# A decoder layer on one core: outer sums by quarters, experts of two tiles side by side, output weights loaded from ScalarE's queue

## The chip, the cores and the metric

The kernel runs on one core of one Trainium2 chip. A core has TensorE (matmuls), VectorE and ScalarE (elementwise work, both read the matmul banks), GpSimd (elementwise work between on-chip buffers) and SyncE, which here only issues DMAs. Each engine works through its own list of instructions in order and waits on semaphores for the others. In the profile they are PE (with PEld for its weight loads), DVE, ACT, POOL and SP. The metric is the device time of one execution in microseconds, lower is better. Everything is float32.

## The reference

The input is 2048 tokens (32 sequences of 64) of 512 numbers. Three blocks follow each other, each on a normalised copy of its input, each added to its input:

```python
# 1: self-attention, 32 heads of 128
q = (hidden_states @ Wq + bq).reshape(b, n, H, HD)      # k, v alike
q = rmsnorm(q, gq); k = rmsnorm(k, gk)
scores = jnp.einsum('bnhd,bmhd->bhnm', q, k) * scale
attn = jax.nn.softmax(scores, axis=-1)
out = jnp.einsum('bhnm,bmhd->bnhd', attn, v).reshape(b, n, H * HD)
return out @ Wo + bo
...
# 2: cross-attention of channels (64 by 64 weights) to a context of 128
energy = jnp.einsum('bcn,bcm->bnm', q, k) / scale
x = jnp.einsum('bnm,bcm->bcn', jax.nn.softmax(energy, axis=-1), v)
return skip + x
...
# 3: 8 of 64 experts
scores = jax.nn.softmax(flat @ router_weight.T + router_bias)
topk_w, topk_idx = jax.lax.top_k(scores, 8)
out = flat * topk_w.sum(-1, keepdims=True) + w_dense @ expert_bias
```

`w_dense` holds the eight chosen weights of a token in a row of 64, zeros elsewhere.

## The kernel before

A tile is 128 tokens (two sequences); there are 16. The big matrix products are computed with Strassen's scheme (Winograd's form): a product of two 2x2 block matrices takes seven block products, numbered 1 to 7, instead of eight, at the price of sums of blocks before and after.

**First half: attention (0 to about 1380 us).** The heads go in 16 groups of two, the tiles in two halves of eight, and of each half two units of four tiles. Two of the group passes (the first group of each half) use one level of the scheme (`single`); the other 30 are *windows* (class `Window`), which use two levels. A window computes q and k of two heads for its two units by four *outer* steps n = 0 to 3, over the outer products (1, 5), (2, 6), (7, 3) and (4,); each outer step runs the seven inner products in up to four places m = 0 to 3 (`outer`, products at L655). VectorE or ScalarE empties a finished bank into the buffer `qk` (first contents L666, L669, L676; additions L679). `qk` of a unit has four places (h, ab) for the two heads and the two kinds of token tile, and in each place j = 0 is q and j = 1 is k. After outer step 2, two *outer sums* bring the places into their final form, `add` at L734: (1, 0) += (1, 1), then (1, 1) += (0, 1), over 128x512, for unit 0 on GpSimd and for unit 1 on VectorE. Outer step 3 then writes over (0, 1). The dictionary `behind` (L737) says after which (n, m) these sums and the squares for the q and k norms (ScalarE, L356) are issued. Between the places m, `plan` puts the value products (`v`, products at L387 into the banks va and vb, copies on ScalarE L403, sums on VectorE L407), the scaling of q and k of the window before (GpSimd L542, VectorE L544), the transposes of the probabilities, and at the end scores (L555), mix (L592) and store (L607) of units already scaled. The weights of the next window are loaded by SP (L107) and their sums made on GpSimd, `more_sums` being the last (L152 to L155), by calls of `make` placed in the dictionary `more`.

In this half the order on VectorE, ScalarE, GpSimd and TensorE is that of the program text. A small list, `waiting`, holds VectorE work (L544, parts of a softmax) that is issued at the next place.

**Passage (about 1380 to 1430).** The attention output of each tile (32 heads of 128) is multiplied by Wo. `load_wo` (L804) brings Wo in eight pieces of 1 MB: the four of its left column at the start of the last window, the four of the right column after it, each as soon as a buffer is free. `wo_sums` makes Wo's block sums in eight steps on VectorE (L860), one at a time, when the generator `making_wo` is advanced. `first_out` is the first pair of tiles: its token sums (L886) are in the dictionary `sums`, by step. `drain` runs the steps: one step is four of the 16 accumulating matmuls of a product, each two instructions (so four steps a product, 28 for the pair); after given numbers of steps it issues the last transposes, scalings and scores of the attention. The last attention units are finished between them.

**Second half: output pairs (about 1430 to 1923).** The other seven pairs run in `strassen_out` (products at L837), again 28 steps a pair; the last pair has its own branch. After each step `advance` moves the *tails* of the pair before on: each tile's cross-attention (`cross_attention`, L1041) and experts (`experts`, L1107) are a generator, and a `yield k` in it means "go on k + 1 steps later". A tail ends with the transpose of the expert weights (L1143), the product with the 64 expert rows (`pm`, L1148, which contracts over 128 rows of which 64 are zero in `eb_sb` and `wds`), an addition (L1149) and the store of the tile (L1150). The odd tile of a pair starts later than the even one. The residual tiles x live in four buffers from their load to their store, so a pair's load of x waits for a store of the pair two before. The matmul banks come from three pools: `ps_a` with three banks (output products, L1095/L1097 and `pm`), `ps_t` with two, `ps_s` with three. In this half only TensorE has the program's order; the others are ordered by the scheduler of the language.

## Time and profile before

| what | us |
|---|---|
| median of 3 runs (1923.52 to 1924.39) | 1923.66 |
| the profiled execution | 1925.16 |
| its span, first to last instruction | 1923.3 |
| TensorE busy | 1878.1 |
| VectorE busy | 1232.1 |
| GpSimd busy | 1042.6 |
| ScalarE busy | 647.7 |
| one window (start to start) | 42.3 |
| one middle output pair (start to start) | 62.26 |

Busy time of TensorE is modelled from the starts of pipelined matmuls, so short refills after a wait count as busy; the distance from start to start is the safer measure. A row of the order in time gives the start in us, the duration, engine, line, operation, result and sources, the shapes and how many instructions were merged; in brackets stand the idle time before it and what ended it. A row of the waits gives who waited for whom, the total, how many times and the longest. The granted TensorE clock is 1.00 of full speed in the windows and in the middle pairs, 0.94 from 1380 to 1430 and 0.93 from 1846 to 1923.

### The profile page before, as it was taken

The page shows a single profiled execution, that of the slowest core. Times are in us where ns is not written, and L with a number is a line of the kernel's source. Part 1 is how long each engine was busy: PE and PEld are TensorE (multiplying, and loading weights), DVE is VectorE, ACT ScalarE, POOL GpSimd, SP SyncE. Part 2 cuts the span into 40 slices and gives each one's busy share as a digit, 9 for nine tenths or more (in the row PEclk, how much of TensorE's full clock was granted, in tenths as well). Part 3 has the DMA queues.
Part 4 walks back from the last instruction along what each step waited for, and adds up shares of the span by engine and source line. Part 5 has one row for each costly group of instructions (what it writes and reads, how often), then busy time and mean ns, then how long its engine had stood idle before and what let it go on. Part 6 is the DMA issues. An engine that isn't in the chain of part 4 may idle for free.

```text
span 1923.3 us, 40481 instructions
## 1 busy us (share of the span) xinstructions
PE 1878.1 (98%) x16845; PEld 1615.8 (84%) x16845; DVE 1232.1 (64%) x2034; ACT 647.7 (34%) x1580; POOL 1042.6 (54%) x814
## 2 busy tenths in 40 slices
PE   9999999999999999999999999999989999999997
PEld 8888888888888888888888888888877888888875
DVE  6866777766666658766666676666663545554555
ACT  2344334344433343344433343443311212221122
POOL 5856666666567639766566766655234323331320
PEclk9999999999999999999999999999999999999998
DMA  4234434333343343333443333344925231223100
GB/s 138 67 125 140 131 113 133 122 105 112 126 130 109 111 143 101 111 100 106 128 132 111 111 109 102 100 127 134 301 74 182 91 111 68 69 91 113 44 25 22
DMA packets 164567, 214.90 MB, mean 112 GB/s; under 512 B 10144, under 2 KB 135136, under 8 KB 160288
## 3 DMA queue, kind: packets, MB, share of 16 engines
q1 hardware_dynamic: 163200, 211.24, 34.1%
q8 instruction: 132, 2.16, 0.5%
q10 hardware_dynamic: 1184, 1.08, 0.2%
q14 instruction: 51, 0.42, 0.1%
HBM read 171.92 MB, written 40.37 MB: 110 GB/s over the span
## 4 chain that ended last, share of the span: by engine, by line
PE 74%; DVE 12%; POOL 7%; issue 3%; DMA 2%; ACT 1%; SPq 0%; POOLq 0%; DVEq 0%; ACTq 0%
PE p_w L655 24%; PE py L837 17%; PE va L387 7%; PE vb L387 6%; POOL qk L734 5%; PE ms_w L779 3%; PE o L592 3%; PE s L555 3%; DVE qk L666 3%; DVE qk L679 3%; DVE qk L544 2%; PE pt_p L249 1%; DMA x<-in_x_dram 1%; PE pa L445 1%; DVE sums L262 1%
## 5 line engine op out<-in xcount | busy, mean ns | idle before, releaser
L655 PE MATMUL p_w<-x,w 128*128 128x256 f32 x2940 | 723.9, 383 | 8.9 <-DVE qk L666 8.4
L655 PEld LDWEIGHTS p_w<-x,w 128*128 128x128 f32 x2940 | 521.2, 190 | 71.0 <-DVE qk L666 13.0
L666 DVE TENSOR_TENSOR qk<-p_w,qk 128x512 f32<-128x512 f32 x360 | 212.7, 599 | 136.5 <-PE p_w L655 100.6
L356 ACT ACTIVATE sq<-qk 128x512 f32<-128x512 f32 x256 | 158.1, 628 | 399.2 <-POOL qk L734 225.1
L387 PEld LDWEIGHTS va<-w,x 128*128 128x128 f32 x2048 | 263.6, 191 | 30.5 <-ACT v L403 20.5
L387 PE MATMUL va<-w,x 128*128 128x128 f32 x2048 | 276.1, 278 | 2.1 <-ACT v L403 2.1
L679 DVE TENSOR_TENSOR qk<-p_w,qk 128x512 f32<-128x512 f32 x360 | 220.1, 620 | 58.4 <-PE p_w L655 54.9
L120 POOL TENSOR_TENSOR w<-w 128x768 f32<-128x768 f32 x126 | 245.3, 1958 | 2.4
L265 POOL TENSOR_TENSOR prob<-prob,inv 128x512 f32<-128x512 f32 x64 | 78.7, 1230 | 298.2 <-DVE inv L264 295.0
L542 POOL TENSOR_TENSOR qk<-qk,rs 128x512 f32<-128x512 f32 x128 | 174.6, 1364 | 101.7 <-DMA rs<-row_w 89.3
L837 PE MATMUL py<-wo,a 128*128 128x256 f32 x992 | 227.5, 381 | 0.4 <-DVE wo L860 0.4
L837 PEld LDWEIGHTS py<-wo,a 128*128 128x128 f32 x992 | 183.7, 190 | 32.3 <-issue 7.3
L387 PEld LDWEIGHTS vb<-w,x 128*128 128x128 f32 x1536 | 201.4, 192 | 9.7
L387 PE MATMUL vb<-w,x 128*128 128x128 f32 x1536 | 202.4, 275 | 0.0
L403 ACT COPY v<-va 128x256 f32<-128x256 f32 x256 | 95.0, 371 | 311.7 <-PE va L387 311.5
L544 DVE SCALAR_TENSOR_TENSOR qk<-qk,gqk,rs 128x512 f32<-128x512 f32 x128 | 171.7, 1342 | 3.9 <-DMA rs<-row_w 2.3
L837 PE MATMUL py<-wo_t,a 128*128 128x256 f32 x672 | 154.7, 381 | 0.0
L837 PEld LDWEIGHTS py<-wo_t,a 128*128 128x128 f32 x672 | 125.2, 190 | 17.3 <-issue 0.8
L734 POOL TENSOR_TENSOR qk<-qk 128x512 f32<-128x512 f32 x60 | 90.7, 1512 | 61.1 <-DVE qk L679 58.7
L407 DVE TENSOR_TENSOR v<-vb,v 128x256 f32<-128x256 f32 x192 | 80.7, 420 | 45.7 <-PE vb L387 27.2
L257 DVE TENSOR_REDUCE mx<-s 128x8 f32<-128x512 f32 x64 | 44.1, 689 | 96.4 <-PE s L555 96.4
L607 ACT ACTIVATE ot<-o,bvt 128x256 f32<-128x256 f32 x256 | 99.4, 470 | 2.2 <-PE o L592 2.2
(193 smaller groups left out, 2227.5 us busy)
## 6 DMA issues: line engine op xcount, KB each, us to landing
rs<-row_w SPq DMA_DIRECT2D x120, 512.0 KB
mixed<-ot SPq DMA_DIRECT2D x64, 512.0 KB
a<-mixed SPq DMA_DIRECT2D x32, 1024.0 KB
w<-in_wq_dram SPq DMA_DIRECT2D x64, 256.0 KB
w<-in_wk_dram SPq DMA_DIRECT2D x62, 256.0 KB
w<-in_wv_dram SPq DMA_DIRECT2D x62, 256.0 KB
wo<-in_wo_dram SPq DMA_DIRECT2D x8, 1024.0 KB
x<-in_x_dram SPq DMA_DIRECT2D x20, 256.0 KB
```

The costliest lines, as they stand in the source:

```text
L120: on.tensor_tensor(*(it.rearrange("p c j d -> p (c j) d") for it in (out, a, b)), ALU.subtract)
L356: nc.scalar.activation(sq, of, AF.Square)
L387: nc.tensor.matmul(to[:, j, :], left[i][:, c, j, :], right[i][:, c, 2, :], start=first and j == 0 and c == 0, stop=c == 1, skip_group_chec ...
L403: nc.scalar.copy(self.v[h, ab], what)
L542: nc.gpsimd.tensor_tensor(k, k, rk, ALU.mult)
L544: lambda: nc.vector.scalar_tensor_tensor(q, q, gqk, rq, ALU.mult, ALU.mult)
L607: nc.scalar.activation(ot[:, h, :, b * SEQ : (b + 1) * SEQ], o[b][:, h, :, :], AF.Identity, bias=bvt[:, hg * HG + h : hg * HG + h + 1],)
L655: nc.tensor.matmul(bank[:, s, :], self.w.inner[o][i], inner_x[self.half, o][i], start=first and s == 0, stop=True, skip_group_check=True,)
L666: nc.vector.tensor_tensor(to(t, j), bank, add(t, j), ALU.add)
L679: nc.vector.tensor_tensor(to(t, j), bank, to(t, j), ALU.add)
L734: on.tensor_tensor(qk[to], qk[to], qk[what], ALU.add)
L837: nc.tensor.matmul(py, a[:, g, :], b[g // KH][:, g % KH, :], start=n == 0 and g == 0, stop=n == last and g == NHG - 1,)
```

## The change

Outer sums: each sum is cut by j into two of 128x256, and each is issued at a place of its own. For unit 0 (GpSimd) the j = 0 pair comes after (2, 1) and the j = 1 pair after (2, 2); for unit 1 (VectorE) the four quarters are spread over (2, 2), (2, 3) and (3, 0). The squares of the second head move back by up to one place. In the windows, the last two calls of `make` move from (2, 3) to (3, 0), and in the windows of group 1 one call of `inner` from (2, 1) to (2, 2).

Passage: the eight loads of Wo are issued by ScalarE instead of SP. Wo's sums are formed in another order (t2 from the new b12, then t1 from t2) and issued after the steps 8, 10, 14, 15, 16, 18, 21 and 22 instead of 9 to 16. In the first pair, product 6 comes before product 5, the token sums are formed with other operands, the addition of product 1 to xa moves behind product 2, and the transposes and scalings are issued after other numbers of steps.

Output pairs: the pair sums on GpSimd (L1008, L1009, in the last pair L969) move to VectorE. Six of the small loads before the first pair (`xw` of v and skip, router weights and bias, and the expert rows, now loaded twice, into rows 0 to 63 and 64 to 127) are issued by ScalarE; the two memsets of GpSimd fall away. The tails have other yields. For the first seven pairs, the even tile stops after it has chosen its experts and the odd tile does the rest for both: one transpose of both tiles' weights side by side (128 x 128), two products over 64 rows each, two additions, two stores. The tiles of the last pair each do their own, over 64 rows.

```diff
@@ -216,6 +216,10 @@
         tc.keep_in_program_order(nc.sync.dma_start(out=to, in_=what))
+    def load_beside(to, what):
+        nc.scalar.dma_start(out=to, in_=what)
     def statistics(xs, name, on_gpsimd=False):
...
@@ -728,25 +732,34 @@
...
                 )
-            def add(t, to, what):
-                qk = units[t].qk
+            def add(t, j, to, what):
+                to, what = (units[t].qk[it][:, j, :] for it in (to, what))
                 on = nc.vector if t else nc.gpsimd
-                on.tensor_tensor(qk[to], qk[to], qk[what], ALU.add)
+                on.tensor_tensor(to, to, what, ALU.add)
             behind = {
                 (1, 3): lambda: [squares(0, 0, t) for t in range(2)],
+                (2, 1): lambda: (
+                    add(0, 0, (1, 0), (1, 1)),
+                    add(0, 0, (1, 1), (0, 1)),
+                ),
                 (2, 2): lambda: (
-                    add(0, (1, 0), (1, 1)),
-                    add(0, (1, 1), (0, 1)),
-                    squares(1, 0, 0),
+                    add(0, 1, (1, 0), (1, 1)),
+                    add(0, 1, (1, 1), (0, 1)),
+                    add(1, 1, (1, 0), (1, 1)),
                 ),
                 (2, 3): lambda: (
-                    add(1, (1, 0), (1, 1)),
+                    add(1, 1, (1, 1), (0, 1)),
+                    add(1, 0, (1, 0), (1, 1)),
+                    squares(1, 0, 0),
                     squares(1, 1, 0),
+                ),
+                (3, 0): lambda: (
+                    add(1, 0, (1, 1), (0, 1)),
                     squares(1, 0, 1),
                 ),
-                (3, 0): lambda: add(1, (1, 1), (0, 1)),
                 (3, 1): lambda: squares(1, 1, 1),
...
@@ -803,10 +816,11 @@
...
             it = it.rearrange("p (g f) -> p g f", f=DH)
-            nc.sync.dma_start(
+            nc.scalar.dma_start(
                 out=it,
...
@@ -861,12 +875,14 @@
...
             for half in range(2):
-                subtract(t1[half], b12[half], b11[half])
-                yield
                 subtract(b12[half], b22[half], b12[half])
...
             for half in range(2):
-                subtract(t2[half], b22[half], t1[half])
+                nc.vector.tensor_tensor(t2[half], b12[half], b11[half], ALU.add)
+                yield
+            for half in range(2):
+                subtract(t1[half], b22[half], t2[half])
                 yield
...
@@ -886,9 +902,9 @@
...
         sums[3] = combine(ALU.add, s1, a21, a22)
-        sums[4] = combine(ALU.subtract, a21, a11, a21)
-        sums[5] = combine(ALU.subtract, a11, s1, a11)
-        sums[6] = combine(ALU.subtract, s4, a12, a11)
+        sums[4] = combine(ALU.subtract, a11, s1, a11)
+        sums[5] = combine(ALU.subtract, s4, a12, a11)
+        sums[7] = combine(ALU.subtract, a21, a22, a11)
         def product(i, it):
...
@@ -900,26 +916,26 @@
...
         nc.scalar.copy(p1, py)
-        nc.gpsimd.tensor_tensor(la, la, p1, ALU.add)
         yield
...
         add(la, py)
+        nc.gpsimd.tensor_tensor(la, la, p1, ALU.add)
         yield
...
         add(lb, py)
-        add(rb_, py)
-        yield
-        py = yield from product(5, s1)
-        add(ra, py)
         add(rb_, py)
...
             nc.gpsimd.tensor_tensor(to, to, p1, ALU.add)
+        yield
+        py = yield from product(5, s1)
+        add(ra, py)
+        add(rb_, py)
         add_bias(xa)
...
@@ -966,7 +982,7 @@
...
             nc.vector.tensor_tensor(s2, s1, a11, ALU.subtract)
-            nc.gpsimd.tensor_tensor(a21, a11, a21, ALU.subtract)
+            nc.vector.tensor_tensor(a21, a11, a21, ALU.subtract)
             py = yield from product(2, a12)
...
@@ -1005,9 +1021,9 @@
...
         nc.vector.tensor_tensor(lb, lb, py, ALU.add)
-        nc.gpsimd.tensor_tensor(a22, a21, a22, ALU.add)
-        nc.gpsimd.tensor_tensor(a21, a11, a21, ALU.subtract)
-        yield
+        nc.vector.tensor_tensor(a22, a21, a22, ALU.add)
+        yield
+        nc.vector.tensor_tensor(a21, a11, a21, ALU.subtract)
         py = yield from product(1, a11)
...
@@ -1038,7 +1054,8 @@
...
         done(tb, xb)
-    def cross_attention(t, xt):
+    def cross_attention(t, xt, apart):
         name = f"x{t}"
@@ -1052,7 +1069,7 @@
...
         nc.scalar.copy(kvs, kv)
-        yield 1
+        yield apart
         halves = [slice(b * SEQ, (b + 1) * SEQ) for b in range(2)]
...
@@ -1104,10 +1121,12 @@
...
         nc.vector.tensor_tensor(xt, xt, py, ALU.add)
+    chosen_by = {}
     def experts(t, xt):
...
         xn = layernorm(xt, name)
-        yield 4
+        yield 3
         ft = work.tile([P, KC, P], F32, tag="ft", name=f"ft_{name}", bufs=1)
...
@@ -1132,27 +1151,44 @@
...
         nc.vector.tensor_tensor(chosen, lg, rest, ALU.not_equal)
-        wd = wds[:, t % 2, 0:NEXP]
+        alone = t >= NT - 2
+        side = 0 if alone else t % 2
+        if side:
+            wds, other = chosen_by.pop(t - 1)
+        else:
+            wds = work.tile([P, 2, NEXP], F32, tag="wds", name=f"wds_{name}")
+        wd = wds[:, side, :]
         nc.vector.scalar_tensor_tensor(wd, ex, inv, chosen, ALU.mult, ALU.mult)
...
         nc.vector.scalar_tensor_tensor(xt, xn, ws, xt, ALU.mult, ALU.add)
-        yield 4
+        if not alone and not side:
+            chosen_by[t] = wds, xt
+            return
+        yield 3
+        n = NEXP if alone else 2 * NEXP
         pw = ps_t.tile([P, P], F32, tag="pt", name=f"pw_{name}")
-        nc.tensor.transpose(pw, wds[:, t % 2, :], ident)
+        nc.tensor.transpose(pw[0:n, :], wds.rearrange("p a e -> p (a e)")[:, 0:n], ident)
         wt = work.tile([P, P], F32, tag="wt", name=f"wt_{name}")
-        nc.scalar.copy(wt, pw)
+        nc.scalar.copy(wt[0:n, :], pw[0:n, :])
         yield 1
-        pm = ps_a.tile([P, D], F32, tag="pa", name=f"pm_{name}")
-        nc.tensor.matmul(pm, wt, eb_sb, start=True, stop=True)
-        nc.vector.tensor_tensor(xt, xt, pm, ALU.add)
-        nc.sync.dma_start(out=out_flat[bass.ts(t, P), :], in_=xt)
+        both = [(t, xt)] if alone else [(t - 1, other), (t, xt)]
+        pms = [ps_a.tile([P, D], F32, tag="pa", name=f"pm{i}_{name}") for i in range(len(both))]
+        for i, pm in enumerate(pms):
+            rows = slice(i * NEXP, (i + 1) * NEXP)
+            nc.tensor.matmul(pm, wt[rows, :], eb_sb[rows, :], start=True, stop=True)
+        for (at, it), pm in zip(both, pms):
+            nc.vector.tensor_tensor(it, it, pm, ALU.add)
+            nc.sync.dma_start(out=out_flat[bass.ts(at, P), :], in_=it)
     def after_attention(t, xt):
-        if t % 2 and t < NT - 1:
-            yield 2
-        yield from cross_attention(t, xt)
+        second = t % 2 and t < NT - 1
+        if second:
+            yield 0
+        yield from cross_attention(t, xt, 3 if second else 1)
         yield from experts(t, xt)
@@ -1346,7 +1382,7 @@
...
                 (1, 3): [lambda: make(1)],
-                (2, 3): [lambda: make(2)],
+                (3, 0): [lambda: make(2)],
             }
...
@@ -1360,7 +1396,7 @@
...
                     ((1, 2), 4),
-                    ((2, 1), 4),
+                    ((2, 2), 4),
                 ):
...
@@ -1434,14 +1470,14 @@
...
                     sums[done]()
-                elif done >= 9:
-                    next(making_wo, None)
-
-        go(2)
+                elif done in (8, 10, 14, 15, 16, 18, 21, 22):
+                    next(making_wo)
+        go(3)
         line.turn()
...
         line.scale()
-        go(4)
+        go(3)
         line.scale()
...
@@ -1475,17 +1511,15 @@
...
             half = slice(b * SEQ, (b + 1) * SEQ)
-            load(xw[half, j, half], src)
+            (load if j < 2 else load_beside)(xw[half, j, half], src)
     rwt = work.tile([P, KC, NEXP], F32, tag="rwt", name="rwt", bufs=1)
-    load(rwt, rw_t.rearrange("(kc p) e -> p kc e", p=P))
+    load_beside(rwt, rw_t.rearrange("(kc p) e -> p kc e", p=P))
     rb_b = work.tile([P, NEXP], F32, tag="rb", name="rb_b", bufs=1)
-    load(rb_b, rb.partition_broadcast(P))
+    load_beside(rb_b, rb.partition_broadcast(P))
     eb_sb = work.tile([P, D], F32, tag="eb", name="eb_sb", bufs=1)
-    wds = work.tile([P, 2, P], F32, tag="wds", name="wds", bufs=1)
-    nc.gpsimd.memset(eb_sb[NEXP:P, :], 0.0)
-    nc.gpsimd.memset(wds, 0.0)
-    load(eb_sb[0:NEXP, :], eb)
+    for half in range(2):
+        load_beside(eb_sb[half * NEXP : (half + 1) * NEXP, :], eb)
     for n in range(6):
...
```

## The prediction

> **What bounds the kernel now.** I read the page first, then the waits, then the order in time of one late window, of the passage between the two halves of the kernel, and of the last pair.
>
> ```profile
> span 1923.3 us, 40481 instructions
> ...
> PE 1878.1 (98%) x16845; PEld 1615.8 (84%) x16845; DVE 1232.1 (64%) x2034; ACT 647.7 (34%) x1580; POOL 1042.6 (54%) x814
> ```
>
> TensorE is busy 98% of the span, so a faster VectorE, ScalarE or GpSimd is worth only the gaps it closes in TensorE's row. The busy sum leaves 45 us, and short refills after a wait hide a little more. The waits of the weight loads show the gap that repeats:
>
> ```profile
> PEld va L387 <- ACT v L403: 20.5, 60, 1.5
> PEld p_w L655 <- DVE qk L666: 13.0, 31, 1.0
> ```
>
> There are 30 windows, so 60 and 31 waits are two and one in each. TensorE's order of time in one window:
>
> ```profile
> 1285.37 1.03 PE L655 MATMUL p_w<-x,w 128*128 128x256 f32 x4
> 1286.36 1.16 PE L387 MATMUL va<-w,x 128*128 128x128 f32 x8
> 1287.74 1.13 PE L655 MATMUL p_w<-x,w 128*128 128x256 f32 x4 [0.22 <-DVE qk L666]
> 1288.72 1.16 PE L387 MATMUL va<-w,x 128*128 128x128 f32 x8
> 1289.72 1.03 PE L655 MATMUL p_w<-x,w 128*128 128x256 f32 x4
> 1290.58 1.05 PE L387 MATMUL vb<-w,x 128*128 128x128 f32 x8
> ```
>
> Read the starts. Undisturbed, four p_w take 0.87 from start to start and eight v products 0.89, so from 1285.37 to 1290.58 the rows need 4.39; they take 5.21. The loss is 0.82 us, 0.49 of it ahead of 1287.74. What stands there, on VectorE and on GpSimd:
>
> ```profile
> 1285.41 0.69 DVE L734 TENSOR_TENSOR qk<-qk 128x512 f32<-128x512 f32 x1
> 1287.26 0.42 DVE L666 TENSOR_TENSOR qk<-p_w,qk 128x256 f32<-128x256 f32 x1 [1.16 <-POOL qk L734]
> ```
>
> ```profile
> 1284.12 3.11 POOL L734 TENSOR_TENSOR qk<-qk 128x512 f32<-128x512 f32 x2 [2.16 <-DVE qk L679]
> 1287.19 1.00 POOL L152 TENSOR_TENSOR w<-w 128x384 f32<-128x384 f32 x1
> ```
>
> GpSimd's two outer sums end at 1287.23; only then may L666 overwrite what they read, and TensorE needs the bank that L666 empties.
>
> **A. Outer sums by quarters (30 windows).** Each 128x512 sum becomes two of 128x256. GpSimd pays a little more (rows of 128x256 on it follow each other every 0.70: L960, three in 2.09), so 2.8 for 3.1 with less waiting. Its first two quarters move in front of the last products of the window's third group, into its idle 2.16. The later two start at 1284.1 as now, behind one VectorE quarter, and end near 1285.75. ScalarE's squares move behind the value copies, so the two short waits of va (0.12 and 0.11) go: copies no longer queue behind squares. VectorE now has three quarters (0.42 each, half of L734's 0.69 with its fixed part) in front of L666, where it had one 0.69.
>
> Here the Trainium skill is weighed. By the nearest row, L734 on VectorE ran its full-speed 0.69 in the middle of GpSimd's sums, which paid instead (3.11 for twice 1.28). If quarters do likewise, L666 comes at about 1286.7, before TensorE needs it, and the whole 0.82 is won: 24.6. "SBUF — State Buffer", section "Who interferes with whom", speaks against it: a VectorE instruction with two SBUF inputs and a GpSimd one that reads SBUF exclude each other for the whole instruction. Then they alternate: quarter two waits for GpSimd's fourth (to 1285.75), ends at 1286.0; L152, which waits for nothing, goes next, to 1286.87; quarter three ends at 1287.15; L666 ends at 1287.55 and TensorE goes on at 1287.6, not at 1287.13. Left are 0.47 and a 0.11 refill: 0.82 − 0.58 = 0.24 a window, 7.2 in all. Other rows side with the rule: of two L886 of equal size the second took 3.01 for 2.25 when a GpSimd prob product (2.90 for 1.04) came between. I take 7.2. Moving the last weights' sums one place (L152's group) costs and brings nothing: no GpSimd instruction stands between the two places.
>
> **B. Passage to the output (1380 to 1430).**
>
> ```profile
> 1426.59 1.55 PE L555 MATMUL s<-qk 128*64 128x64 f32 x24 [5.15 <-DVE qk L544]
> ```
>
> ```profile
> 1415.91 1.53 DVE L544 SCALAR_TENSOR_TENSOR qk<-qk,gqk,rs 128x512 f32<-128x512 f32 x1
> 1417.37 5.55 DVE L860 TENSOR_TENSOR wo_t<-wo,wo_t 128x2048 f32<-128x2048 f32 x2
> ...
> 1425.71 0.74 DVE L544 SCALAR_TENSOR_TENSOR qk<-qk,gqk,rs 128x512 f32<-128x512 f32 x1
> ```
>
> The last scores wait for L544, which stands behind eight output-weight sums (L860, 2.28 each) in VectorE's order. The change spreads these over steps 8 to 22, so five, not eight, stand ahead: three less are 6.8, over the wait of 5.15. The slow rows after it (24 scores 1.48 for 0.81, mix products 1.91 for 1.09) go with it: 6.6 in all, of which I leave 0.6 as a rest. The exchange of products 5 and 6 puts each behind its own sum and adds no instruction.
>
> Against this stand the eight 1 MB loads, now in ScalarE's order. Today SP issues three of the second four at 1370 to 1376 and the last at 1386:
>
> ```profile
> 1370.24 6.46 SPq L809 DMA_DIRECT2D wo<-in_wo_dram  x3
> ...
> 1386.58 0.40 SPq L809 DMA_DIRECT2D wo<-in_wo_dram  x1
> ```
>
> On ScalarE all four follow the last store's copies, which end at 1384.07. "DMA: Bandwidth & Descriptors", section "Issuing engines are not separate DMA queues", says that a second issuer saves only issue time. By SP's issue rows alone the change would save 0.5 of queue ahead of x; by the rule 4 MB and 1.75 MB of rs, bo and x share what now carries 2.75: at the 301 GB/s of 1388 to 1394 they end near 1405, where x now lands at 1396.9. Product 3 (from 1397.6) needs the first two loads, there near 1393 and 1399: hidden. The first sum needs the third, near 1402 (now 1398.2), and the L544 of the earlier scores stands behind it: about 1.0. The first four loads add four issues of about 0.45 (ScalarE's own issue rows at the start, 0.39 to 0.63), 1.9 us ahead of the bias and value copies of the last window; those banks are wanted again some 3.7 later. Without that cover it costs 1.9 once. So B is 6.6 − 0.6 − 1.0 = 5.0, between −4 (product 3 waits too) and 6.6.
>
> **C. First output pairs.** SP no longer issues six small loads ahead of ct:
>
> ```profile
> 1465.15 0.46 PE L1050 MATMUL kv<-ct,wqk 128*128 128x128 f32 x2 [1.73 <-DMA ct<-in_ctx_dram]
> ```
>
> This and the 0.36 ahead of 1460.13 go: 2.1, between 0 and 2.1. ScalarE does no other work from 1442 to 1460, which hides its issues.
>
> **D. Experts side by side (seven pairs).** Removed a pair: one transpose (0.11 from start to start) and one of two 0.86 mixtures; the two left contract 64 rows each. Not shown before; the nearest row is L1097, two products on half the array, 1.01 and some 0.15 of change-over: 1.17 for 1.72. That is 0.55 + 0.11 = 0.66, 4.6 in all; 0 if they run one after the other, 6.8 if they fully overlap. Cost: the pools of three banks. Pair 0's tail is five steps late in pair 2, so its two mixtures meet there a full bank waiting for x (this pair's x load waits for the same output) and the bank of the running product. The second waits until the first is added: 1.75 from mixture to end of add (1520.92 to 1522.67), about 1.5 net; if it takes the bank that waits for x, until L1004: 8.4. Net 3.1. In other pairs both outputs leave at step 29 rather than 28 and 31, x comes up to 3 us later, and VectorE waits for it in L1004 (3.5 now); the bank is wanted only about 24 after the pair's start and is free near 12, which hides it. The pair sums L1008 and L1009 on VectorE (2.28 each, 4.5 on GpSimd) fall in its idle time; the other moved yields only shift work inside full TensorE time.
>
> **E. Last pair.** L969 moves to VectorE:
>
> ```profile
> 1826.54 6.28 DVE L968 TENSOR_TENSOR a_s<-a_s,a 128x2048 f32<-128x2048 f32 x1
> ```
>
> 6.28 becomes 2 x 2.28, so the norms behind it come 1.7 earlier. TensorE's waits of 1.58 and 1.93 follow from one delay: 1.7, not both; between 0 and 3.5.
>
> **F. The tail.** The second-last tile's mixture leaves the place between the last one's transposes and logits (about 0.65), and one more add stands before the last norm: 0.3, between −1 and 1.5.
>
> **Sum:** 7.2 + 5.0 + 2.1 + 3.1 + 1.7 + 0.3 = 19.4. The profiled execution took 1925.16, 1.9 more than its span: span 1903.9, time 1905.8; its distance of 1.5 to the median 1923.66 taken off, **1904**. A change of 0.2% (3.8 us) is about what a measurement tells from none.
>
> **Rivals.**
> 1. Windows lose nothing more (A is 24.6): 1887. For it: the undelayed L734. Against: its good luck was a start between two GpSimd sums.
> 2. The waits move: the bank in pair 2 costs 8.4 and the weights are 2 later than I say: 1904 + 6.9 + 2 = 1913. For it: 4 MB issued 8 to 14 later; against: any freed bank will do.
> 3. Slower: one more GpSimd sum (1.00) gets in front of L666 in every window, A is (0.24 − 1.00) x 30 = −22.8: 1904 + 30 = 1934. It decides from the point where the window loses 0.41 more than today (12.2 of other gains over 30). Against: two GpSimd sums must pass between two VectorE ones.
> 4. Quarters and side-by-side mixtures do nothing (A 0, mixtures serial): 1904 + 7.2 + 4.6 = 1916.
>
> **How the numbers follow.** Forecast 0.45 (own range 1898 to 1909), rival 1 0.25, rival 2 0.12, rival 4 0.09, rival 3 0.09. The range 1884 to 1917 leaves out rival 3 and the far side of rival 1. Faster 0.90; of rival 3 I give 0.02 to within 0.2%, and 0.08 to slower.
>
> **What would show it.** Right: L387 no longer waits for L403; window period near 42.1 (41.5 in rival 1, over 43 in rival 3) for 42.3; scores of the passage within 1 us; no ct wait; a middle pair at 61.6 for 62.26. Wrong: L666 late behind a VectorE quarter, a wait of several us at a mixture in pair 2, or product 3 of the first pair waiting for wo.

## The result, and the profile after

The changed kernel takes 1919.25 us (median of 11 runs, 1912.78 to 1921.32), the kernel before, run beside it, 1924.98 (11 runs): a ratio of 0.9967, 95% interval 0.9957 to 0.9977. It is faster by 0.33%, about 6 us. The forecast was 1904, and its range ended at 1917: direction right, two thirds of the gain missing. The profiled execution took 1920.47 us, its span is 1918.7.

The page of the changed kernel, its head and the engines' busy time:

```profile
span 1918.7 us, 40515 instructions
...
PE 1870.7 (97%) x16838; PEld 1618.0 (84%) x16838; DVE 1256.2 (65%) x2107; ACT 652.3 (34%) x1573; POOL 1008.5 (53%) x859
```

TensorE still bounds the kernel, and its busy sum fell by 7.4 us. The waits of the changed kernel (who waited for whom: total, times, longest):

```profile
PEld p_w L659 <- DVE qk L670: 12.1, 26, 0.5
...
PE p_w L659 <- DVE qk L670: 8.1, 27, 0.9
```

L659 and L670 are L655 and L666 of before. The 60 waits of va for ScalarE's copies are gone from this list but for one; the wait of p_w for VectorE is smaller and still there. The order in time of a late window, TensorE:

```profile
1316.65 1.03 PE L659 MATMUL p_w<-x,w 128*128 128x256 f32 x4
1317.52 1.05 PE L391 MATMUL va<-w,x 128*128 128x128 f32 x8
1318.86 1.13 PE L659 MATMUL p_w<-x,w 128*128 128x256 f32 x4 [0.28 <-DVE qk L670]
1319.82 1.05 PE L391 MATMUL va<-w,x 128*128 128x128 f32 x8
1320.71 1.03 PE L659 MATMUL p_w<-x,w 128*128 128x256 f32 x4
```

From 1317.52 to 1318.86 stand 1.34 us where 0.89 is needed. The gain can be placed by the same five stretches in both traces (from the starts of the sums of squares `ms`, of the first output product, of the first e_x and of the last kv; from the last `ms` to the first output product stand 4.41 us in both). The changed kernel's passage holds the odd tile's first kv product too, 0.45 us, which stood in the pairs before.

| stretch | before | after | won | forecast |
|---|---|---|---|---|
| start to the squares of the last window but one | 1334.77 | 1323.43 | 11.3 | A: 7.0 |
| last window | 42.33 | 47.07 | −4.7 | 0.2 |
| passage, to the first e_x | 87.71 | 87.66 | 0.05 | B and C: 7.1 |
| pairs, to the last kv | 423.48 | 419.12 | 4.4 | D and E: 4.8 |
| tail, to the end | 30.6 | 37.0 | −6.4 | F: 0.3 |

Windows brought more than was forecast and pairs nearly what was forecast. Nothing came out of the passage, and two stretches that the forecast had at about zero lost 11 us. At the last window stands ScalarE; the order in time of ScalarE and its DMA issues (ACTq) in the changed kernel:

```profile
1328.55 0.38 ACTq L823 DMA_DIRECT2D wo<-in_wo_dram  x1
...
1328.97 0.59 ACTq L823 DMA_DIRECT2D wo<-in_wo_dram  x1
...
1329.59 2.15 ACTq L823 DMA_DIRECT2D wo<-in_wo_dram  x1
...
1331.79 5.12 ACTq L823 DMA_DIRECT2D wo<-in_wo_dram  x1
1336.95 0.84 ACT L673 ACTIVATE qk<-p_w,bqd 128x256 f32<-128x256 f32 x2 [6.55 <-issue]
```

The first issue takes 0.38 us and the fourth 5.12, and ScalarE computes nothing meanwhile. TensorE at the same time:

```profile
1337.84 1.13 PE L659 MATMUL p_w<-x,w 128*128 128x256 f32 x4 [3.63 <-ACT qk L673]
1338.81 1.50 PE L391 MATMUL va<-w,x 128*128 128x128 f32 x8
```

It waits 3.63 for a bank and then works at half clock for a while (va takes 1.50 for 1.05).

In the tail it is the clock. A table of stretches of the changed kernel (time, length, then busy time of PE, PEld, DVE, ACT, POOL with counts, the granted TensorE clock, DMA share and GB/s):

```profile
1882.00:1885.40 3.40, 1.18 (x18) 1.02 (x17) 1.38 (x4) 0.81 (x3) 0.79 (x2) 1.00 0.41 154
1885.40:1888.80 3.40, 3.40 (x12) 0.94 (x8) 1.49 (x4) 1.53 (x9) 0.00 (x0) 0.50 0.00 0
1888.80:1892.20 3.40, 0.54 (x4) 0.00 (x0) 2.18 (x5) 1.37 (x8) 1.00 (x2) 1.00 0.00 0
1892.20:1895.60 3.40, 2.55 (x12) 2.36 (x13) 1.32 (x3) 1.16 (x2) 0.12 (x1) 0.50 0.00 0
1895.60:1899.00 3.40, 3.40 (x12) 2.16 (x10) 1.24 (x8) 1.03 (x4) 0.00 (x0) 0.50 0.00 0
1899.00:1902.40 3.40, 3.05 (x7) 0.88 (x7) 1.53 (x4) 0.26 (x1) 0.00 (x0) 0.50 0.00 0
```

A stretch in which TensorE was mostly idle is followed by one at half clock. From 1892.2 to the end the clock stays at 0.50.

### The profile page after: what moved, and what is told of

Its sections match the earlier page's. It is cut to its first block, busy times and chain, and to the rows that moved or that the text cites. A ratio compares the mean times of both kernels' runs of the same rounds, so it can differ in the third digit from the quotient of the medians.

```text
span 1918.7 us, 40515 instructions
## 1 busy us (share of the span) xinstructions
PE 1870.7 (97%) x16838; PEld 1618.0 (84%) x16838; DVE 1256.2 (65%) x2107; ACT 652.3 (34%) x1573; POOL 1008.5 (53%) x859
## 4 chain that ended last, share of the span: by engine, by line
PE 84%; DVE 6%; POOL 4%; DMA 3%; issue 2%; ACT 1%; ACTq 0%; SPq 0%; POOLq 0%; DVEq 0%
PE p_w L659 30%; PE py L851 17%; PE va L391 10%; PE vb L391 7%; PE ms_w L792 3%; PE o L596 3%; PE s L559 3%; DVE qk L670 1%; PE pt_p L253 1%; PE pa L449 1%; PE py_x L1114 1%; PE e_x L1077 1%; DVE qk L739 1%; PE py_x L1112 1%; PE pl_f L1135 1%
## 5 line engine op out<-in xcount | busy, mean ns | idle before, releaser
L659 PE MATMUL p_w<-x,w 128*128 128x256 f32 x2940 | 724.7, 383 | 13.5 <-DVE qk L670 8.1
L659 PEld LDWEIGHTS p_w<-x,w 128*128 128x128 f32 x2940 | 521.7, 191 | 75.2 <-DVE qk L670 12.1
L391 PEld LDWEIGHTS va<-w,x 128*128 128x128 f32 x2048 | 268.8, 192 | 14.7 <-ACT v L407 1.8
L670 DVE TENSOR_TENSOR qk<-p_w,qk 128x512 f32<-128x512 f32 x360 | 212.4, 598 | 94.1 <-PE p_w L659 92.7
L391 PE MATMUL va<-w,x 128*128 128x128 f32 x2048 | 270.4, 275 | 1.4 <-ACT v L407 1.4
L548 DVE SCALAR_TENSOR_TENSOR qk<-qk,gqk,rs 128x512 f32<-128x512 f32 x128 | 170.9, 1335 | 2.0 <-DMA rs<-row_w 1.3
L976 POOL TENSOR_TENSOR x<-x,p 128x256 f32<-128x256 f32 x42 | 42.8, 1038 | 174.5 <-ACT p L1029 77.5
L739 POOL TENSOR_TENSOR qk<-qk 128x256 f32<-128x256 f32 x120 | 103.4, 863 | 10.5 <-DVE qk L683 5.8
```

The source lines that it names most:

```text
L391: nc.tensor.matmul(to[:, j, :], left[i][:, c, j, :], right[i][:, c, 2, :], start=first and j == 0 and c == 0, stop=c == 1, skip_group_chec ...
L548: lambda: nc.vector.scalar_tensor_tensor(q, q, gqk, rq, ALU.mult, ALU.mult)
L659: nc.tensor.matmul(bank[:, s, :], self.w.inner[o][i], inner_x[self.half, o][i], start=first and s == 0, stop=True, skip_group_check=True,)
L670: nc.vector.tensor_tensor(to(t, j), bank, add(t, j), ALU.add)
L739: on.tensor_tensor(to, to, what, ALU.add)
```

## The experiments

All runs are compared with the kernel before on the same chip. The changed kernel is 0.9967 on that scale; 0.001 is 1.9 us.

| run | what it is | median us | ratio to before, 95% interval |
|---|---|---|---|
| quarters_only | before, A alone | 1916.19 | 0.9949 (0.9933 to 0.9965) |
| passage_only | before, B without ScalarE's queue | 1918.98 | 0.9967 (0.9955 to 0.9979) |
| before_wo_act | before, first four Wo loads on ScalarE | 1930.12 | 1.0023 (1.0014 to 1.0031) |
| experts_only | before, D and F alone | 1929.60 | 1.0019 (1.0008 to 1.0031) |
| vector_sums_only | before, E alone | 1922.68 | 0.9987 (0.9978 to 0.9996) |
| wo_on_sp | after, all Wo loads on SP | 1909.19 | 0.9905 (0.9888 to 0.9921) |
| wo_first_on_sp | after, first four on SP | 1913.66 | 0.9943 (0.9929 to 0.9957) |
| small_on_sp | after, C undone | 1915.60 | 0.9950 (0.9937 to 0.9963) |
| adds_later | after, three additions later | 1917.68 | 0.9962 (0.9949 to 0.9975) |
| gate | after, L152 made to wait | 1903.15 | 0.9887 (0.9871 to 0.9902) |
| fill | after, one gap of the tail filled | 1919.31 | 0.9961 (0.9946 to 0.9975) |
| busy_tail | after, four gaps filled | 1912.28 | 0.9934 (0.9920 to 0.9949) |
| best1 | after, four edits | 1889.71 | 0.9814 (0.9800 to 0.9829) |
| best_tail | best1, pair 6 each tile by itself | 1889.14 | 0.9813 (0.9797 to 0.9828) |
| best_busy | best1 and busy_tail | 1883.73 | 0.9785 (0.9769 to 0.9800) |

### The loads of Wo

```diff
 # wo_on_sp; wo_first_on_sp has (nc.sync if n == 0 else nc.scalar)
-            nc.scalar.dma_start(
+            nc.sync.dma_start(
                 out=it,
 # before_wo_act, in the kernel before
-            nc.sync.dma_start(
+            (nc.scalar if n == 0 else nc.sync).dma_start(
                 out=it,
```

> The changed kernel with one part undone: SP issues the eight loads of Wo, as before the change. Theory (the issues block ScalarE): the last window, 47.07 us from its squares to the next in the changed kernel, goes back to about 42.0, the row of ScalarE's bias copies no longer stands 6.55 behind an issue, and the time falls by about 5 us, to 1914. Rival (the last window is late for another reason, or what it gains is waited for in the passage behind it): the last window stays near 47, or it comes down and the passage gives it back; the time stays within 1.5 us of 1919.

> The kernel before with one part of the change alone: the first four loads of Wo, those at the start of the last window, are issued by ScalarE; the second four stay with SP. Theory: ScalarE stands some 7 us in the four issues, TensorE waits for a bank, and the last window is 4.5 to 5.5 us longer; the time is about 1930. Rival (the block comes only together with other parts of the change): the issues take 0.4 to 0.6 each, and the time stays within 1.5 us of 1925.

> The changed kernel with SP issuing the first four loads of Wo; ScalarE keeps the second four. Theory (each four loads cost by themselves: 5.5 in the last window, the rest of the 10 us in the passage): the last window is 41.5 in place of 47.07, the waits of 2.31 at the scores and of 2.27 for xw stay, and the time is 1913 to 1914.5. Rival (the second four cost nothing, all comes from the first): the time is 1909 to 1910, as in the run wo_on_sp.

Undone, the last window is 41.50 long, not 47.07, and the stretch from the first output product to the first e_x 80.66, not 87.66: 5.6 and 7.0 us in the traces. By the ratios (0.9967 to 0.9905) all eight loads cost 12 us, uncertain by some 4. The expectation of 5 was less than half of it: the passage loses as much as the window, and the rival, that what is won would be given back, is out. On the kernel before, the same four loads bring back the same rows (ScalarE in before_wo_act):

```profile
1341.99 5.09 ACTq L809 DMA_DIRECT2D wo<-in_wo_dram  x1
1347.12 0.84 ACT L669 ACTIVATE qk<-p_w,bqd 128x256 f32<-128x256 f32 x2 [6.35 <-issue]
```

They cost 0.23% (4.4 us) there with nothing else changed. So the block needs no other part of the change. With the first four loads on SP and the second four on ScalarE the time is 1913.66, close to the forecast, though the last window is 43.54 (another wait of 1.76 for L670 comes in). The passage takes 85.11, so that 4.45 of its 7.0 are the second four loads. The other 2.5 stand at xw, which waits 2.27 in the changed kernel with half clock behind it, and 1.5 without half clock here. The second four in wo_first_on_sp, ScalarE first, then VectorE and TensorE:

```profile
1372.70 0.70 ACTq L823 DMA_DIRECT2D wo<-in_wo_dram  x1
...
1378.73 1.67 ACTq L823 DMA_DIRECT2D wo<-in_wo_dram  x2
1380.44 0.58 ACT L582 COPY probt<-pt_p 128x512 f32<-128x512 f32 x1 [6.25 <-DMA wo<-in_wo_dram]
```

```profile
1391.56 3.27 DVE L874 TENSOR_TENSOR wo<-wo,wo 128x2048 f32<-128x2048 f32 x1 [2.89 <-DMA wo<-in_wo_dram]
1394.75 0.74 DVE L548 SCALAR_TENSOR_TENSOR qk<-qk,gqk,rs 128x512 f32<-128x512 f32 x1
```

```profile
1395.64 0.92 PE L559 MATMUL s<-qk 128*64 128x64 f32 x24 [2.20 <-DVE qk L548]
```

Between the second issue and the third, ScalarE stands until other DMAs have landed. In the trace the DMAs of SP and ScalarE share eight semaphores that tell of landings, and an issue begins only when the last DMA on its semaphore has landed. The third issue starts 0.02 us after SP's load of `rs`, with the same semaphore, has landed (1378.71), the fourth 0.02 us after the first of these loads has (1379.63). ScalarE's copy of the last transposed probabilities (L582) stands 6.25 us behind them, but no TensorE row waits for it. What TensorE loses comes by way of the data: the third load lands at 1391.53, VectorE's first sum of Wo starts then, and L548 and the scores stand behind it. From the first output product to the mix behind these scores the two traces differ by 2.4 us; another 1.6 comes at the pt_p wait of 2.64, which stands in both traces and has half clock behind it only here.

### Where L666 still waits

```diff
-                (3, 0): [lambda: make(2)],
+                (3, 0): [lambda: gate(), lambda: make(2)],
             }
+            def gate(units=units):
+                seen = small.tile([P, 8], F32, tag="gate", name=f"gate_{n}")
+                of = units[1].qk[1, 0][:, 0, 0:8]
+                nc.gpsimd.tensor_tensor(seen, of, of, ALU.add)
```

> The changed kernel with one small instruction more on GpSimd in each window: it adds eight elements of a row that VectorE's third quarter writes, so that the weights' last four sums (L152 to L155) start only behind that quarter. Theory (GpSimd's L152 gets between VectorE's second and third quarter and keeps TensorE waiting 0.48 a window): the two quarters take 1.08 in place of 1.89, the wait of p_w for qk goes, the window is 41.55 to 41.65 in place of 42.05, and the time falls by 11 to 14 us, to about 1906. Rival (the quarters are late for the banks anyway, or the weights' sums now end too late for the next window): the window stays at 42.0 or gets longer, and the time is 1919 or more.

The window goes from 42.05 to 41.51 and the wait of p_w for L670 from 8.1 us in 27 waits to 1.7 in 2. The ratio falls by 0.8%, 15 us, a little more than the 11 to 14 expected. VectorE and GpSimd, first in the changed kernel:

```profile
1316.57 1.89 DVE L739 TENSOR_TENSOR qk<-qk 128x256 f32<-128x256 f32 x2
1318.39 0.41 DVE L670 TENSOR_TENSOR qk<-p_w,qk 128x256 f32<-128x256 f32 x1
```

```profile
1317.01 1.18 POOL L152 TENSOR_TENSOR w<-w 128x384 f32<-128x384 f32 x1
```

and in the kernel of the run gate:

```profile
1260.24 1.09 DVE L739 TENSOR_TENSOR qk<-qk 128x256 f32<-128x256 f32 x2
1261.26 0.41 DVE L670 TENSOR_TENSOR qk<-p_w,qk 128x256 f32<-128x256 f32 x1
```

```profile
1261.41 0.20 POOL L1391 TENSOR_TENSOR gate<-qk 128x8 f32<-128x8 f32 x1 [0.70 <-DVE qk L739]
1261.57 1.00 POOL L152 TENSOR_TENSOR w<-w 128x384 f32<-128x384 f32 x1
```

Two VectorE quarters take 1.89 where a GpSimd sum of two on-chip operands stands between them and 1.09 where it is held back by 0.20 us of work. The changed kernel has a control of its own: the last window of the first half has no weights' sums behind it, and it is 41.51 long.

### The parts alone

> The kernel before with part A alone: the outer sums by quarters, the squares and the weights' last sums moved with them. Theory (A is worth what the two traces show): a window is 42.05 in place of 42.34 in 28 windows, the last one about 41.5, together 8 to 10 us, and nothing behind the windows takes it back: about 1916.5. Rival (the gain of A is lost again at the end of the windows, where the weights of Wo are waited for): the windows are shorter, but the output pairs start no earlier and the time stays above 1922.

> The kernel before with the reordered sums of Wo, the reordered first pair and the other numbers of steps alone (part B without ScalarE's queue). Theory: the wait of 5.15 for VectorE's scaling goes, with its slow rows 6 to 6.6 us; the 2.64 us wait for GpSimd's prob product behind three additions comes instead, so that 3 to 4 us are left: about 1922. Rival (the chain of B is worth nothing, since another late sum takes the place): a wait of 4 us or more stands at the scores or at a py, and the time stays within 1.5 us of 1925.5.

> The kernel before with part D alone: two tiles' expert weights side by side, the other yields, the expert rows loaded twice; all loads stay with SP, and the pair sums stay on GpSimd. Theory (D saves in the pairs and, since pair 6 leaves no mixture for the tail's gap, costs the clock at the end): a pair is 61.7 in place of 62.26, some 3 us less up to the last pair, but from the last kv to the end 36 to 37 us in most executions in place of 30.6: about 1927, slower than before. Rival (the tail's clock goes by where in time the gaps fall, not by this part): the tail stays near 31, and the time is about 1922.

> The kernel before with part E alone: the pair sums on VectorE. Theory: in the last pair L968 takes 2.3 in place of 6.28, the waits of 1.58 and 1.93 at e_x shrink by 1.7 together, and nothing else moves: about 1923.5. Rival (VectorE has no room in the middle pairs): 2.3 us sums stand ahead of the additions that free TensorE's banks, a pair gets longer than 62.26 by 0.1 or more, and the time is 1925 or above.

These runs take whole parts of the diff into the kernel before. quarters_only: 42.05 in all windows with weights' sums behind them, 0.51% won, as its theory said. passage_only: 0.33% won, more than the 3 to 4 expected; from the first output product to the first e_x it takes 81.07 for 87.71. The 5.15 wait is gone, and the 2.64 at pt_p is there.

experts_only is slower by 0.19%. The time from the last kv to the end is 36.0 in its profile for 30.6; its passage is 2.1 longer as well (89.85), which was not looked into. Its pairs are not worth what was expected either: from the second e_x of pair 1 to the last kv it takes 416.22 for 416.56, while E alone takes 414.60 and the changed kernel 412.65. A middle pair in the changed kernel is 61.69 long for 62.26; the two mixtures side by side, and the one that waits for its bank in pair 2:

```profile
1693.52 1.13 PE L1182 MATMUL pm_f<-eb_sb,wt_f 64*128 64x512 f32 x4
```

```profile
1519.29 1.12 PE L1182 MATMUL pm_f<-eb_sb,wt_f 64*128 64x512 f32 x2 [0.78 <-DVE x L1184]
```

In pair 2 of experts_only one product waits besides, and loses 1.03 us from start to start against the same place in the changed kernel:

```profile
1546.41 1.56 PE L1098 MATMUL py_x<-att_x,kvs 128*64 128x512 f32 x4 [0.48 <-ACT att_x L1093]
```

vector_sums_only wins 0.13% (2.5 us), a little more than its theory.

### The tail and the clock

```diff
+    def keep_busy(count):
+        idle = ps_a.tile([P, D], F32, tag="pa", name=f"idle_{nc.get_next_instruction_name()}")
+        for _ in range(count):
+            nc.tensor.matmul(idle, ident, eb_sb, start=True, stop=True)
...
         nc.scalar.copy(kvs, kv)
+        if t == NT - 1:
+            keep_busy(2)            # fill: only this one
...
         nc.vector.tensor_tensor(xt, xt, py, ALU.add)    # end of cross_attention
+        if t == NT - 2:
+            keep_busy(3)
...
+        if t == NT - 1:
+            keep_busy(1)            # behind the logits
...
+        if t == NT - 2:
+            keep_busy(2)            # behind the mixture
```

> The changed kernel with two products more that nobody reads, put between the last tile's kv products and the wait of 2.22 us for its norm, about 2.1 us of work for TensorE. Theory (with nothing to do there TensorE loses its clock, and the tail then runs at half speed): the granted clock holds until the next gap of 3.71, the time from the last kv to the end falls from 37.0 to 31 to 33, and the kernel's time by 4 to 6 us, to about 1914. Rival (the clock is granted by something longer than this gap, such as the power of the whole kernel): the clock in the tail stays at 0.50 to 0.72 and the time at 1919, or up to 1 us above it.

> The changed kernel with products that nobody reads in all four larger gaps of the tail, not only in the first as in fill: two (1.88 us at full clock) in the gap of 2.22, three in that of 3.71, two in that of 2.69 and one in that of 1.76. Theory (TensorE loses its clock when a stretch of some 3.4 us is mostly idle, wherever it begins): no such stretch is left, the granted clock stays at 1.00 to the last mixture, the time from the last kv to the end is 29 to 31 in place of 37.0, the kernel takes 1911 to 1913, and the times of single executions lie closer together than the 8.5 us of the changed kernel. Rival (the half clock comes from elsewhere, a budget of power for instance): the products run at half clock too and delay the tail; 1919 to 1925.

fill missed: 1919.31, no change. In its profile the clock held over the filled gap, fell behind the next one of 3.71 and came back 6.9 us later. With all four gaps filled the kernel takes 1912.28, 7 us less (6.4 by the ratios), its five runs lie within 3.7 us (11 of the changed kernel within 8.5), and its tail takes 30.1 for 37.0. The same kind of table for busy_tail:

```profile
1882.90:1886.30 3.40, 2.90 (x22) 1.62 (x22) 1.47 (x4) 0.90 (x3) 0.79 (x2) 1.00 0.41 154
1886.30:1889.70 3.40, 3.40 (x17) 1.23 (x14) 2.38 (x6) 1.57 (x9) 0.00 (x0) 1.00 0.00 0
1889.70:1893.10 3.40, 2.47 (x11) 1.19 (x10) 2.62 (x7) 1.34 (x8) 1.12 (x2) 1.00 0.00 0
...
1900.00:1903.40 3.40, 1.89 (x10) 0.91 (x9) 0.55 (x1) 0.58 (x1) 0.74 (x2) 1.00 0.22 80
1903.40:1906.80 3.40, 3.20 (x9) 1.39 (x8) 2.08 (x10) 0.60 (x3) 0.00 (x0) 0.51 0.00 0
```

No stretch is idle enough until the one from 1900.0. So idle TensorE, not a budget, takes the clock. Products that nobody reads add work and save 6 to 7 us.

How far the change itself is to blame is seen from the time between the last kv and the end in one profile each. With the tail of before: 30.6, 31.0, 32.7, 32.7, 33.2 (before, quarters_only, passage_only, before_wo_act, vector_sums_only; mean 32.0). With the tail of the change and no filling: 37.0, 31.9, 36.0, 34.5, 37.0, 35.4, 36.0, 32.0 (after, wo_on_sp, wo_first_on_sp, small_on_sp, adds_later, gate, experts_only, best1; mean 35.0). By these few profiles some 3 us go with the structure; the rest is when the gaps fall, as the single times of one kernel show (wo_on_sp: 1902.85 to 1912.23).

### The rest of the passage

```diff
 # adds_later
         add(p1, py)
+        yield
         for to in (ra, lb, rb_):
             nc.gpsimd.tensor_tensor(to, to, p1, ALU.add)
-        yield
 # small_on_sp
-            (load if j < 2 else load_beside)(xw[half, j, half], src)
+            load(xw[half, j, half], src)
 # and load for load_beside at rwt, rb_b and eb_sb
```

> The changed kernel with the three GpSimd additions behind product 6 issued after the next step, so that GpSimd's prob product goes first. Theory (the prob product stands behind additions[...]): the wait of 2.64 at pt_p goes, with about 1 us of slow clock behind it, and the time is about 1915.5. Rival (the additions now hold up the sums of the first pair or the x behind them): another wait of 2 us or more comes in before e_x, and the time stays at 1918 to 1920.

> The changed kernel with part C undone: all small loads ahead of the first output pair are issued by SP again. Theory (C is worth its 2.1, though the wait for xw hides a part): ct is waited for again, 1 to 2 us, and the time is 1920 to 1921.5. Rival (C brings nothing, since the loads that count, those of xw for q and k, stand behind the same three loads of a on SP either way): no change, 1918.5 to 1919.5.

What the first is about, in the changed kernel (TensorE, then GpSimd):

```profile
1426.80 0.66 PE L253 MATMUL pt_p<-ident,prob 128*128 128x128 f32 x4 [2.64 <-POOL prob L269]
```

```profile
1419.52 6.22 POOL L934 TENSOR_TENSOR x<-x,p 128x256 f32<-128x256 f32 x3 [10.29 <-DVE p L915]
1425.70 1.04 POOL L269 TENSOR_TENSOR prob<-prob,inv 128x512 f32<-128x512 f32 x1
```

VectorE makes two sums of Wo from 1420.19 to 1425.16 (4.97 us), and three GpSimd additions on 128x256 that take 2.1 by the rate of such rows in the kernel before (L960, three in 2.09) take 6.22. With the additions moved the wait is gone from the trace, but a py then waits 1.95 for `a`, and the ratio, 0.9962 for 0.9967, tells nothing: its rival is as near as its theory. In best1, where the loads are in order too, neither wait is left.

With C undone the kernel is not slower; 0.9950 against 0.9967, with intervals that overlap. The wait for ct is back (1.48), the wait for xw (2.27) gone. Why, SP's order shows; in the changed kernel and then in small_on_sp:

```profile
1434.83 8.84 SPq L835 DMA_DIRECT2D a<-mixed  x3
```

```profile
1434.01 2.65 SPq L835 DMA_DIRECT2D a<-mixed  x3
```

ScalarE issues its small loads from 1434.5 to 1440.0, and xw for q and k stand behind the three loads of `a` on SP. The row of 8.84 is not issue time: single issues take 1.79, 0.32 and 0.32, and between them SP waits. The waits of SP from 1430 to 1450 in the changed kernel, and from 1401.6 to 1428.6 in best1:

```profile
SPq L835 <- DMA a<-mixed: 3.7, 1, 3.7
SPq L835 <- DMA bo_b<-in_bo_dram: 2.6, 1, 2.6
```

```profile
SPq L835 <- DMA xw<-in_xwq_t_dram: 6.0, 1, 6.0
```

The loads of `a` read neither bo_b nor xw. The semaphores of landings explain it: ScalarE's loads take six of the eight meanwhile, so the second `a` has to wait for that of bo_b and the third for that of the first. At these loads such waits stand in all ten traces in which ScalarE issues small loads of this place, and in none of the seven others. The landings themselves are no slower: the first `a` lands 8.5 us after the start of its issue, 8.6 in small_on_sp.

### A version from the pieces

```diff
 # best1: wo_on_sp, gate and adds_later, and
-            (load if j < 2 else load_beside)(xw[half, j, half], src)
+            load_beside(xw[half, j, half], src)
 # best_tail: the same, and
-        alone = t >= NT - 2
+        alone = t >= NT - 4
 # best_busy: best1 and the four keep_busy of busy_tail
```

> The changed kernel with four edits: Wo's loads back on SP; the small GpSimd instruction of the run named gate; the first pair's three GpSimd additions of product 6 one step later, behind the prob product; all small loads of the cross-attention on ScalarE. Theory: the gains of wo_on_sp (10) and gate (16) add up, the wait of 2.64 and the wait of 1.4 to 2.3 for xw go: 1886 to 1892. Rival (they close the same gap, or the additions' new place makes product 5's sums late): 1895 or more.

> The kernel of the run best1, with the last pair but one (tiles 12 and 13) doing its experts each by itself as the last pair does, so that a mixture again lies between the last kv and the last e_x. Theory (when the gaps fall, not what was taken from them, sets the clock): two transposes and two short mixtures in place of one and two, about 0.3 us more; between 1889 and 1892. Rival (the mixture taken from the gap sets the clock): the tail is shorter by 2 us or more in the median, below 1888.

> The kernel of the run best1 with the same unread products in the tail. Theory: 31.8 us from the last kv to the end become 29 to 31, and 1889.7 becomes 1886 to 1888. Rival: best1 has its clock in the tail anyway, in nearly all executions, and the products only delay the first work behind a gap: 1889 to 1892.

best1 is within its theory, 1.9% faster than before. best_tail can't be told from it: its theory holds, though best1 had little to win back, since its profiled tail takes 32.0 already. best_busy, with 1883.73 us 2.15% faster than before, is the fastest kernel run here and came out below its forecast of 1886 to 1888.

## Why the prediction was wrong, by its steps

**A, 7.2: right, and a little small.** A window of 42.05 against a forecast of 42.1; alternation was right: L666 stands behind a GpSimd sum between VectorE quarters, and the rule of the Trainium skill ("SBUF — State Buffer", "Who interferes with whom") decided it against the row of L734. What the run gate adds: rival 1's window of 41.5 was there to be had, at 41.51, by one waiting instruction. Of the 11.3 in the table, 2.8 lie ahead of the first window's squares, where before has a stretch at half clock (10.4 to 13.8) and after none. The other 8.5 are 0.29 in each of 25 windows, 0.8 in the last window of the first half, and 1.0 between the halves (93.97 from squares to squares for 95.01), less 0.6 in the first window.

**B, 5.0: the mechanism was right, the loads were mis-sized.** Three sums fewer ahead of L544, worth 6.6: passage_only has 6.64 in that stretch. Two terms failed:
- "The first four loads add four issues of about 0.45", 1.9 us under a cover of 3.7. They took 0.38, 0.59, 2.15 and 5.12, 8.2 together, ended far past the cover, and cost 4.4 (before_wo_act) to 5.6. ScalarE's rows "at the start, 0.39 to 0.63", were of loads of 256 KB and less, with no 1 MB loads ahead of them. The kernel before had a sign of it, in SP's row of the third and fourth of the same loads, 0.98 each:

```profile
1344.30 1.95 SPq L809 DMA_DIRECT2D wo<-in_wo_dram  x2
```

The row of three in 6.46 is no such sign: its single issues took 0.37 to 0.38, and SP waited between them for buffers that TensorE was still reading. In the seven traces with the first four on ScalarE the fourth issue ends 0.60 to 0.77 after the first load has landed; what holds it until then stays open.
- For the second four the forecast had 1.0: a late first sum, with L544 of the earlier scores behind it. That path was right and its size too small. It cost 2.4 in wo_first_on_sp, and half clock at a later wait 1.6 more; all four together 4.45 by the traces. The forecast let ScalarE issue the four in one go. In fact the third issue stood some 6 us behind the second, until a DMA of SP had landed.

The rule used there, "DMA: Bandwidth & Descriptors", "Issuing engines are not separate DMA queues", holds as far as it goes: nothing was faster for a second issuer. The issue time that it calls usually small beside the DMA was 5.12 us here (the first of these loads landed 7.6 after its issue began), taken from a computing engine.

**C, 2.1: wrong.** The ct wait went as forecast, and another stood in its place: xw, 2.27, behind `a` loads on SP that were out after 8.84 in place of 2.65. The forecast had counted the issues that C takes from SP's queue and nothing for the waits that it brings there, 6.3 us until other DMAs had landed.

**D, 3.1: sizes near, result smaller.** 0.57 a pair for 0.66; in pair 2 the second mixture waited for the first one's bank, as the cheaper of the two cases said (54.95 from e_x to e_x for 53.62, 1.3 for 1.5). **E, 1.7:** 1.96 in its own run. D and E together 3.9 in the changed kernel for 4.8; D alone 0.3, so that most of D is only there when the pair sums are on VectorE. Of the 1.6 missing there, 1.03 is the wait for att_x in pair 2; the rest was not looked into.

**F, 0.3 between −1 and 1.5: wrong, 6.4 lost between the two profiles, some 3 in the mean of several.** The step counted instructions and left the clock out. Without the mixture TensorE idles 2.22 for 0.81 between kv and e_x, one more gap that can cost the clock. fill shows that this gap alone was not the cause; busy_tail that the gaps together were.

**The sum.** By the runs of parts, A 9.8, B without loads 6.4, E 2.5, D and F −3.7; the Wo loads −12 (0.9967 to 0.9905): 3.0 against the 6.4 measured (0.33%), C left out; each of the five is uncertain by 2 to 4 us, so the sum closes only within some 6. What the forecast's range left out was two losses at once, of 11 us together, in the last window and in the tail, both costed at about nothing, and a passage that won nothing.

## What to carry to other kernels

A DMA put into the queue of an engine that computes is an instruction of that engine: cost it by the issue rows of loads of that size with others still under way, and ask what the engine does next. Ask too which landings an issue has to wait for, also on the other issuer; a row of several issues holds the waits between them. Where two elementwise engines take turns on on-chip operands, look for the one unhurried instruction that gets between two hurried ones, and make it wait. In a tail with little work, TensorE's gaps cost twice, and products that nobody reads can be cheaper than idling.

## What was not expected of the hardware

- **The clock has a grid.** In each profile the granted clock changed only at points a whole number of 3.41 us apart. In before it falls at 10.4 and at 1901.4, which is 554.0 times 3.4133; in quarters_only at 9.2 and 1893.4, 552.0 times. The grid doesn't begin with the execution (first fall at 8.6 to 11.1 in 13 of the 17 profiles), so the same gap costs nothing in one execution and a stretch of half clock in the next: the wait of 2.64 at pt_p has half clock behind it in the changed kernel and none in wo_on_sp. The Trainium skill says so ("TensorE: Matmul & The Clock Gate", Part 1: a free-running window of 3.4 us). Counted over the stretches of this grid that ran at full clock in the 17 profiles, from 20 us on: every one in which TensorE was busy for less than 1.50 us was followed by half clock, none with more than 1.92 was, and between the two both occur.
- **Getting the clock back can take longer than one busy stretch.** The same section lets the clock return after one busy window. wo_on_sp got it back after a stretch with 2.74 of 3.40 busy; the changed kernel, at half clock, had 2.55, 3.40 and 3.05 busy in three stretches running and did not. What is counted as busy there stays open; the logits, eight products of 64 columns, lie in the 3.40.
- **A short wait elsewhere costs the clock too.** The last window's wait of 3.63 was followed by half clock from 1339.2 to 1342.7, the wait of 2.64 at pt_p by one from 1428.0 to 1431.4. Each adds up to 1.7 us to the wait itself.
